# Graph attention on one core: q and k kept token by token, first loads amid the projections, keys loaded in eight parts

## The chip, the cores and the metric

The kernel runs on one core of a Trainium2 chip. The metric is the device time of one execution in microseconds (us), from the first to the last work of the core. A profiled execution gives the trace; its own time stands beside its span below, since all durations in the text come from it.

## The reference: what is computed

There are two layers on a graph of 2708 nodes with 128 features. Nearly all of the time goes into the first one, an attention whose 128 "batches" come from a plain reshape:

```python
q = (x @ Wq.T).reshape(d, n, h)        # d = 128, n = 2708, h = 8
k = (x @ Wk.T).reshape(d, n, h)
v = (x @ Wv.T).reshape(d, n, h)
a = jnp.einsum('dnh,dmh->dnm', q, k) * scale
a = a + spatial_encoding + edge_encoding   # both are adj
a = jax.nn.softmax(a, axis=2)
out = jnp.einsum('dnm,dmh->dnh', a, v).reshape(n, h * d)
x = _layernorm(x + out @ Wo.T)
```

Because of the reshape, batch d does not take one feature of every node. The projection's rows are laid end to end as 2708 x 128 rows of 8 numbers, and each batch takes 2708 consecutive ones, that is, rows of about 21 and a bit consecutive tokens. The second layer is a graph convolution, `adj @ (x @ W2) + b2` and once more with `W4`, with a residual and a layer norm.

## The kernel before

**Projections (L180 to L210).** The 2708 tokens go in 22 blocks of up to 128. For each block TensorE computes k, q and v (two matmuls of 512 columns each, L196). For k and q, ScalarE writes the value rounded to float32r (L205) and VectorE the rest, value minus rounded value (L206), so that both halves together keep the precision; the tile `pr` holds both. One DMA on SyncE's queue stores it (L208) into `ks` or `qs`. These DRAM tensors have 16 rows (8 numbers of the first half, 8 of the second) of 346624 = 2708 x 128 elements each, so that a token's data are 16 pieces of 128 elements, 512 bytes, far apart. v goes to `vs`, 4096 bytes in one piece per token (L201). For a later test of the range, VectorE takes the maximum and the minimum of each row (L210). The pool of `pr` has four buffers, so two blocks are under way.

**Attention (L213 to L443).** A group g is four of the 128 batches; there are 32 groups. In a group, the 2708 queries go in 6 blocks b of 452 (`QBS`), and for each block the 22 chunks of 128 keys are worked off in 9 steps (`plan`), for all four batches at once. A step has 2 to 4 pieces, each of two score tiles in the PSUM tile `s`, and three more score tiles in `p`. The engines share the work:

- TensorE makes the scores (L350, L347) and later multiplies the weights with the values and sums them up in `acc` (L371, L367).
- VectorE adds the adj column tile to `s` (L357), ScalarE takes the exponential of the sum (L443).
- For the tiles in `p`, ScalarE takes the exponential of the score alone (L440) and GpSimd multiplies with the exponential of adj (L441). That is computed once, in group 0 (L338), kept in DRAM (`near_exp`, stored at L339) and loaded afterwards (L328).
- At the end of a block VectorE copies `acc` to `o` (L377), and four DMAs store it (L379).

`interleave` lays out by hand which piece, sum or copy comes next, by times that it estimates; the order of instructions on each engine follows from it (`tc.manual_schedule()`). The projections lie outside of that and are ordered by the framework.

**Loads.** All DMAs are issued from SyncE's queue, in order; it stands still where one of them waits. At the start of each step, SyncE loads adj tiles until it is 8 tiles past what this step needs (L420). There are three kinds: `col` (one tile, 9 buffers), `two` (two tiles, two DMAs, 3 buffers) and `ecol` (7 buffers). Ahead of that, in the fourth step of a block (i == 3), come the 8 DMAs with the queries of the next block (`load_q`, L310; 16 rows each, so that both halves of k meet both halves of q). In step (b, i) = (1, 0) come the keys of the next group:

```python
def load_keys(g):
    t = raw.tile([P, N], F32R, tag="k_raw", name="k_raw")
    for j in range(GB):
        r0 = (GB * g + j) * N
        for i in range(4):
            nc.sync.dma_start(t[ds(32 * j + H * i, H), :].bitcast(F32), ks[ds(H * (i // 2), H), ds(r0, N)])
```

These are 16 DMAs of 8 rows. In step (2, 0) the values follow (`load_values`, 8 DMAs, L302 and L303). From block 2 on, GpSimd reorders them in pieces, one every other step: `order_keys` (L291, 8 pieces, and L295) and `spread_values` (L308). For group 0 all of this, with its memsets (L233 to L239), stands between the projections and the loop (L385 to L391).

**After the loop.** `layer0_out` divides, projects and normalises, and tests that all numbers lay in the range in which the exponentials need no maximum (L568, L569). If they did not, a branch at the end (L630) repeats the attention with maxima (`attention_with_maxima`); with these inputs it is not taken. `layer1` reads adj twice more.

Of the kernel before, what the change touches and what calls it, by code (L numbers as in the profile page):

```python
# [9 lines left out]
F32 = mybir.dt.float32  # L10
# [8 lines left out]
P = 128  # L19
# [110 lines left out]
def graph_attention_gcn(ctx: ExitStack, tc: tile.TileContext, x, xT, adj, adjT, adjP, adjS,  # L130
# [34 lines left out]

    qs = dram.tile([2 * H, R], F32, name="qs")
    ks = dram.tile([2 * H, R], F32, name="ks")
    vs = dram.tile([R, H], F32, name="vs")
# [3 lines left out]

    ends = const.tile([P, 2, 2, NM], F32, name="ends")
    nc.gpsimd.memset(ends, 0.0)

    with ExitStack() as s:
        wpool = s.enter_context(tc.tile_pool(name="wqkv", bufs=1))
        sb = s.enter_context(tc.tile_pool(name="proj", bufs=4))  # L180
        ps = s.enter_context(tc.tile_pool(name="ps_proj", bufs=4, space=PSUM))

        xT_sb = wpool.tile([P, N], F32, name="xT_sb")
        for i0, mi in ((0, P), (P, N - P)):
            nc.sync.dma_start(xT_sb[:, ds(i0, mi)], xT[:, ds(i0, mi)])
        w_sb = []
        for name, w in (("k", WkT), ("q", WqT), ("v", WvT)):
            t = wpool.tile([P, H * P], F32, name=f"w{name}_sb")
            nc.sync.dma_start(t, w)
            w_sb.append(t)  # L190
        v3 = vs.rearrange("(i g) e -> i (g e)", g=P)
        for c, (i0, mi) in enumerate(MC):
            for w, dst in zip(w_sb, (ks, qs, vs)):
                pp = ps.tile([P, 2, 512], F32, tag="pp", name="pp")
                for h in range(2):
                    nc.tensor.matmul(pp[:mi, h, :], xT_sb[:, ds(i0, mi)], w[:, ts(h, 512)], start=True, stop=True)  # L196
                flat = pp[:mi].rearrange("p a b -> p (a b)")
                if dst is vs:
                    o = sb.tile([P, H * P], F32, tag="po", name="po")
                    nc.scalar.copy(o[:mi], flat)  # L200
                    nc.sync.dma_start(v3[ds(i0, mi)], o[:mi])  # L201
                else:
                    f = half_scale if dst is qs else 1.0
                    o = sb.tile([P, 2, H * P], F32R, tag="pr", name="pr")
                    nc.scalar.mul(o[:mi, 0], flat, f)  # L205
                    nc.vector.scalar_tensor_tensor(o[:mi, 1], flat, f, o[:mi, 0].bitcast(F32), ALU.mult, ALU.subtract)  # L206
                    d3 = dst.rearrange("e (i g) -> i e g", g=P)
                    nc.sync.dma_start(d3[ds(i0, mi)], o[:mi].bitcast(F32).rearrange("p l (e g) -> p (l e) g", g=P))  # L208
                    for i, op in enumerate((ALU.max, ALU.min)):
                        nc.vector.tensor_reduce(ends[:mi, int(dst is qs), i, c : c + 1], o[:mi, 0].bitcast(F32), AX.X, op)  # L210


    with ExitStack() as s:  # L213
        kept = s.enter_context(tc.tile_pool(name="kept", bufs=1))
        raw = s.enter_context(tc.tile_pool(name="raw", bufs=1))
        kpool = s.enter_context(tc.tile_pool(name="kpool", bufs=2))
        qpool = s.enter_context(tc.tile_pool(name="qpool", bufs=3))
        cols = s.enter_context(tc.tile_pool(name="cols", bufs=9))
        twos = s.enter_context(tc.tile_pool(name="twos", bufs=3))
        ecols = s.enter_context(tc.tile_pool(name="ecols", bufs=7))  # L220
        epool = s.enter_context(tc.tile_pool(name="weights", bufs=4))
        ppool = s.enter_context(tc.tile_pool(name="products", bufs=4))
        opool = s.enter_context(tc.tile_pool(name="sums", bufs=2))
        ps = s.enter_context(tc.tile_pool(name="ps_s", bufs=2, space=PSUM))
        pq = s.enter_context(tc.tile_pool(name="ps_q", bufs=1, space=PSUM))
        pa = s.enter_context(tc.tile_pool(name="ps_a", bufs=1, space=PSUM))

# [47 lines left out]

        def load_keys(g):

            t = raw.tile([P, N], F32R, tag="k_raw", name="k_raw")
            for j in range(GB):
                r0 = (GB * g + j) * N  # L280
                for i in range(4):
                    nc.sync.dma_start(t[ds(32 * j + H * i, H), :].bitcast(F32), ks[ds(H * (i // 2), H), ds(r0, N)])
            groups[g] = kpool.tile([P, NU, P], F32R, tag="k", name="k"), k_short[g % 2], vals[g % 2], v_short[g % 2]
            raw_keys[g] = t

        def order_keys(g, i):

            t, (k, kz, _, _) = raw_keys[g], groups[g]
            if i < 8:
                n = P // 8  # L290
                nc.gpsimd.tensor_copy(k[:, :, ts(i, n)], t[:, ts(i, n * NU)].rearrange("p (q c) -> p c q", c=NU))  # L291
            else:
                for j in range(GB):
                    r = ds(32 * j, 32)
                    nc.gpsimd.tensor_copy(kz[r, ds(32 * j, SHORT)], t[r, ds(P * NU, SHORT)])  # L295

        def load_values(g):
            t = raw.tile([P, GB, NU * H], F32, tag="v_raw", name="v_raw")
            vz = v_short[g % 2]
            for j in range(GB):  # L300
                r0 = (GB * g + j) * N
                nc.sync.dma_start(t[:, j, :], vs[ds(r0, P * NU), :].rearrange("(p c) e -> p (c e)", c=NU))  # L302
                nc.sync.dma_start(vz[ds(32 * j, SHORT), ds(VW * j, H)], vs[ds(r0 + P * NU, SHORT), :])  # L303
            values[g] = t

        def spread_values(g, j):
            to = vals[g % 2].rearrange("p c (j e) -> p j c e", e=VW)
            nc.gpsimd.tensor_copy(to[:, j, :, :H], values[g][:, j, :].rearrange("p (c e) -> p c e", e=H))  # L308

        def load_q(g, b):  # L310
            n0, nw = QBS[b]
            q = qpool.tile([P, QB], F32R, tag="q", name="q")
            for j in range(GB):
                for i in range(2):
                    nc.sync.dma_start(q[ds(32 * j + 2 * H * i, 2 * H), :nw].bitcast(F32),  # L315
                                      qs[:, ds((GB * g + j) * N + n0, nw)])
            queries[g, b] = q

        def load_adj(n):
# [9 lines left out]
            else:  # L329
                t = adj_cols[g, b, m] = cols.tile([P, QB], F32, tag="col", name="col")  # L330
                m = -1 - m if m < 0 else m
                nc.sync.dma_start(t[:, :nw], adjP[ds(m * P, P), ds(n0, nw)])

        def first_exp(b, m):

            nw = QBS[b][1]
            t = ecols.tile([P, QB], F32, tag="ecol", name="ecol")
            nc.scalar.activation(t[:, :nw], adj_cols[0, b, -1 - m][:, :nw], AF.Exp, scale=2.0)  # L338
            nc.sync.dma_start(near_exp[b, m][:, :nw], t[:, :nw])  # L339
            exp_cols[0, b, m] = t  # L340

        def score(to, g, b, m, j):
            nw = QBS[b][1]
            k, kz, _, _ = groups[g]
            q = queries[g, b]
            if m == NU:
                nc.tensor.matmul(to[:, :nw], kz, q[:, :nw], start=True, stop=True)  # L347
            else:
                r = ds(32 * j, 32)
                nc.tensor.matmul(to[:, :nw], k[r, m, :], q[r, :nw], start=True, stop=True)  # L350

# [31 lines left out]
        s.enter_context(tc.manual_schedule())  # L383
        ahead, loaded = 8, 0
        load_keys(0)  # L385
        load_values(0)
        load_q(0, 0)
        for h in range(9):
            order_keys(0, h)
        for j in range(GB):  # L390
            spread_values(0, j)  # L391
        for what, n, c, beside in interleave(plan, len(steps) // len(plan), NU):
# [10 lines left out]
            if c == 0:  # L403
# [4 lines left out]
                if g + 1 < NG:  # L408
                    if (b, i) == (1, 0):
                        load_keys(g + 1)  # L410
                    elif (b, i) == (2, 0):
                        load_values(g + 1)
                    elif b > 1 and n % 2:
                        h = ((b - 2) * len(plan) + i) // 2
                        if h < 9:
                            order_keys(g + 1, h)
                        elif h < 9 + GB:
                            spread_values(g + 1, h - 9)
# [49 lines left out]
    nc.gpsimd.memset(reach, 1.0)  # L468
    fine = keep.tile([P, 7], F32, name="fine")

# [14 lines left out]
    def layer0_out(sb, ps, pa, judge):  # L485
# [72 lines left out]
        if judge:  # L558
# [4 lines left out]
            for i in range(2):  # L563
                limit = QK_LIMIT * (1.0, half_scale)[i]
                bounds += [(ends[:, i, 0, :], ALU.max, limit, ALU.is_le), (ends[:, i, 1, :], ALU.min, -limit, ALU.is_ge)]
            for i, (a, way, limit, op) in enumerate(bounds):
# [62 lines left out]
    rows_fine = nc.values_load(n_fine, min_val=0, max_val=P)  # L629
    with tc.If(rows_fine < P):  # L630
        with ExitStack() as t:
            attention_with_maxima(t, tc, qs, ks, vs, os_, adj, adjT, ident)
        rest(False)
# [127 lines left out]
```

## Time and profile before

| | us |
|---|---|
| median of 3 runs | 7105.78 |
| lowest and highest run | 7080.25, 7123.37 |
| the profiled execution's own time | 7111.18 |
| its span, first to last instruction | 7109.3 |
| first matmul starts | 8.79 |
| last store of the projections is issued, lands | 200.56, 205.10 |
| first add of the loop (VectorE, L357) starts | 232.62 |
| last copy `o` of the loop (L377) starts | 6771.7 |

The span thus has four stretches: the projections up to 205 us, 27.5 us up to the loop's first add, the loop up to about 6772 us, and some 337 us for the rest. The granted TensorE clock is 0.984 of full speed in the mean. DMA moves 1642.64 MB, 231 GB/s in the mean, in 1118588 packets.

The lines that follow in the prediction are read like this. In the page's first part, an engine has its busy time and share of the span. In its second part the span is cut into 40 slices, and each digit is the busy share in tenths. In the table by stretches, a row has the start and end, the length, the busy time of TensorE, its weight loads, VectorE, ScalarE and GpSimd (with the number of instructions), the granted clock, the mean share of the 16 DMA engines, and the rate. In the timeline a row has the start, the duration, the engine (SPq is SyncE's queue), the line of the kernel, the operation, and what is written from what.

### The profile page before, as it was taken

Reading aid. Unit: us, or ns where it says so; the run is one execution under the profiler, and the core shown is the slowest. Engines: PE = TensorE matmul, PEld = TensorE weight load, DVE = VectorE, ACT = ScalarE, POOL = GpSimd, SP = SyncE. Lnnn points to the kernel's source line nnn. Section 1 sums busy time; section 2 is a strip of 40 time slices with the busy share of each in tenths; the row PEclk is TensorE's granted clock in tenths of the full one; section 3 lists DMA queues with packets and bytes.
Section 4 is the critical chain, followed back from the end, with each engine's and each line's share of the span. In section 5 each row is a group of like instructions: output and inputs, shape, how many; then the busy total and the mean of one; then the engine's idle time right before and its main releaser. Section 6 shows DMA issues by size and latency. Waiting matters only on the chain.

```text
span 7109.3 us, 136670 instructions
## 1 busy us (share of the span) xinstructions
PE 6795.0 (96%) x50426; PEld 2165.0 (30%) x50426; DVE 6148.8 (86%) x6208; ACT 6549.0 (92%) x3659; POOL 5613.7 (79%) x2266
## 2 busy tenths in 40 slices
PE   6599999999999999999999999999999999999979
PEld 2122232323333233222322322223322222333354
DVE  7589999989999899888999988989988898999951
ACT  3699999999999999999999999999999999999920
POOL 0588888888888888888888888888888888888800
PEclk9799999999999999999999999999999999999999
DMA  9777767767766776777667776776667776677667
GB/s 287 224 246 234 233 223 237 245 221 231 236 225 230 236 242 223 227 235 228 222 229 236 242 221 221 232 228 227 229 226 232 230 237 221 226 237 232 227 189 233
DMA packets 1118588, 1642.64 MB, mean 231 GB/s; under 512 B 144373, under 2 KB 1083385, under 8 KB 1113685
## 3 DMA queue, kind: packets, MB, share of 16 engines
q1 hardware_dynamic: 1117908, 1633.81, 70.8%
q8 instruction: 399, 6.54, 0.4%
q14 instruction: 281, 2.29, 0.1%
HBM read 1551.44 MB, written 81.80 MB: 230 GB/s over the span
## 4 chain that ended last, share of the span: by engine, by line
PE 45%; DMA 16%; ACT 11%; DVE 8%; POOL 8%; issue 8%; SPq 3%; DVEq 0%; ACTq 0%; POOLq 0%
PE acc L371 22%; PE s L350 15%; POOL w L441 8%; DVE e L357 7%; ACT e L443 6%; DMA col<-in_adjP 6%; ACT w L440 4%; DMA ecol<-ne 4%; PE acc L588 3%; DMA k_raw<-ks 2%; DMA two<-in_adjP 2%; PE p L350 2%; PE acc L367 2%; SPq L315 1%; DMA ks<-pr 1%
## 5 line engine op out<-in xcount | busy, mean ns | idle before, releaser
L441 POOL TENSOR_TENSOR w<-w,ecol 128x1356 f32<-128x1356 f32 (+1 forms) x1728 | 5351.1, 3103 | 934.4 <-ACT w L440 845.0
L357 DVE TENSOR_TENSOR e<-s,col 128x904 f32<-128x904 f32 (+1 forms) x4608 | 4829.6, 1091 | 499.1 <-PE s L350 182.8
L443 ACT ACTIVATE e<-e 128x2712 f32<-128x2712 f32 (+5 forms) x1728 | 4709.0, 2725 | 2.6 <-DVE e L357 2.5
L371 PE MATMUL acc<-e,vals 128*32 128x452 f32 x21888 | 3844.9, 558 | 11.5 <-ACT e L443 0.6
L350 PE MATMUL s<-q,k 32*128 32x452 f32 x10944 | 2468.4, 468 | 188.8 <-DVE e L357 79.6
L440 ACT ACTIVATE w<-p 128x1356 f32<-128x1356 f32 (+1 forms) x1728 | 2395.4, 1386 | 78.4 <-PE p L350 72.9
L350 PEld LDWEIGHTS s<-q,k 32*128 32x128 f32 x10944 | 1027.4, 183 | 3360.5 <-DVE e L357 2846.9
L371 PE MATMUL acc<-w,vals 128*32 128x452 f32 x10368 | 1671.9, 559 | 0.0
L350 PE MATMUL p<-q,k 32*128 32x452 f32 (+1 forms) x5184 | 1273.4, 439 | 13.3 <-ACT w L440 13.1
L357 DVE TENSOR_TENSOR e<-s,two 128x904 f32<-128x904 f32 (+1 forms) x960 | 1047.6, 1091 | 182.8 <-ACT w L440 80.6
L371 PEld LDWEIGHTS acc<-e,vals 128*32 128x32 f32 x21888 | 621.6, 108 | 857.5 <-issue 789.7
L350 PEld LDWEIGHTS p<-q,k 32*128 32x128 f32 x5184 | 521.4, 183 | 31.9 <-ACT w L440 31.0
L371 PEld LDWEIGHTS acc<-w,vals 128*32 128x32 f32 x10368 | 280.3, 108 | 205.1 <-issue 178.1
L291 POOL CAST k<-k_raw 128x336 fp32r<-128x336 f32 x256 | 225.7, 883 | 13.2 <-DMA v_raw<-vs 13.2
L367 PE MATMUL acc<-e,v_short 128*128 128x452 f32 (+1 forms) x384 | 196.7, 594 | 0.0
L233 POOL MEMSET k_short<- 128x128 f32 x2 | 0.3, 204 | 203.9 <-DMA vs<-po 203.9
L205 ACT ACTIVATE pr<-pp 128x1024 fp32r<-128x1024 f32 (+1 forms) x44 | 45.0, 1023 | 116.0 <-DMA ks<-pr 55.5
L377 DVE COPY o<-acc 128x452 f32<-128x452 f32 x192 | 118.5, 617 | 6.2 <-PE acc L371 6.2
L588 PE MATMUL acc<-col,xw 128*128 128x512 f32 (+2 forms) x264 | 105.6, 549 | 0.0
L588 PE MATMUL acc<-col,hw 128*128 128x512 f32 (+2 forms) x264 | 104.1, 545 | 0.0
L210 DVE TENSOR_REDUCE ends<-pr 128x1 f32<-128x1024 f32 (+1 forms) x88 | 102.7, 1207 | 0.0
L480 ACT ACTIVATE sd<-mv,eps 128x1 f32<-128x1 f32 (+1 forms) x22 | 5.9, 291 | 104.7 <-DVE mv L474 104.7
(77 smaller groups left out, 980.4 us busy)
## 6 DMA issues: line engine op xcount, KB each, us to landing
col<-in_adjP SPq DMA_DIRECT2D x1965, 226.0 KB
two<-in_adjP SPq DMA_DIRECT2D x1440, 226.0 KB
ecol<-ne SPq DMA_DIRECT2D x1395, 226.0 KB
col<-in_adjP SPq DMA_DIRECT2D x393, 224.0 KB
two<-in_adjP SPq DMA_DIRECT2D x288, 224.0 KB
ecol<-ne SPq DMA_DIRECT2D x279, 224.0 KB
col<-in_adjT SPq DMA_DIRECT2D x210, 256.0 KB
k_raw<-ks SPq DMA_DIRECT2D x512, 84.6 KB
```

The costliest lines, as they stand in the source:

```text
L210: nc.vector.tensor_reduce(ends[:mi, int(dst is qs), i, c : c + 1], o[:mi, 0].bitcast(F32), AX.X, op)
L291: nc.gpsimd.tensor_copy(k[:, :, ts(i, n)], t[:, ts(i, n * NU)].rearrange("p (q c) -> p c q", c=NU))
L315: nc.sync.dma_start(q[ds(32 * j + 2 * H * i, 2 * H), :nw].bitcast(F32), qs[:, ds((GB * g + j) * N + n0, nw)])
L350: nc.tensor.matmul(to[:, :nw], k[r, m, :], q[r, :nw], start=True, stop=True)
L357: nc.vector.tensor_add(e[:, ds(at, 2), :nw], st[:, :, :nw], a)
L367: nc.tensor.matmul(a[:, :nw], vz, e[:, t, :nw], start=False, stop=False)
L371: nc.tensor.matmul(a[ds(32 * j, VW), :nw], v[:, m, ds(VW * j, VW)], e[:, t, :nw], start=(m == first_chunk), stop=(m == last_chunk))
L377: nc.vector.tensor_copy(o[:, :nw], acc.pop((g, b))[:, :nw])
L440: nc.scalar.activation(w[:, :, :nw], sp[:, :, :nw], AF.Exp, scale=2.0)
L441: nc.gpsimd.tensor_mul(w[:, :, :nw], w[:, :, :nw], exp_cols[g, b, two][:, :nw].unsqueeze(1).to_broadcast([P, 3, nw]))
L443: nc.scalar.activation(e[:, :at, :nw], e[:, :at, :nw], AF.Exp, scale=2.0)
L588: nc.tensor.matmul(acc[:, :nw], src[:mw, m, :], t[:mw, :nw], start=(m == 0), stop=(last is None and m == NM - 1))
```

## The change

In words:

- `qs` and `ks` become `[N, 16, 128]`: each token's 16 pieces lie together, 8192 bytes. The projection stores a token in one piece.
- The loads of k and q read whole tokens, from the one that holds the first wanted row to the one that holds the last (`whole_tokens`). They read 16 or 8 pieces of 512 bytes per token and put the tokens side by side, shifted so that the wanted part begins at element 128 of the tile. The tiles grow: `k_raw` from 2708 to 24 x 128 elements per partition, `q` from 452 to 768. `qpool` goes from three buffers to two.
- Group 0's keys (8 parts, blocks 2 to 9), its first queries and its values (blocks 10 to 13), and its first eight adj tiles (blocks 14 to 17) are loaded inside the projections' loop; GpSimd's reordering for group 0 follows there too, and the memsets come ahead of the projections. The loop begins with `loaded = ahead`, 8. The pools `weights`, `products`, `sums` and the PSUM pools open after the projections' pools have closed.
- In later groups the keys come in eight parts of two DMAs, in steps 0 to 7 of block 1; the values in four parts, in steps 0, 2, 4 and 6 of block 2.
- For the range test, one reduction of absolute values takes the place of maximum and minimum, and two bounds the place of four.
- The first 128 columns of xT and the weights are loaded ahead of the rest of xT.
- The branch that is not taken first copies `qs` and `ks` into the old layout.

```diff
-    qs = dram.tile([2 * H, R], F32, name="qs")
-    ks = dram.tile([2 * H, R], F32, name="ks")
+    qs = dram.tile([N, 2 * H, P], F32, name="qs")
+    ks = dram.tile([N, 2 * H, P], F32, name="ks")
...
-        qpool = s.enter_context(tc.tile_pool(name="qpool", bufs=3))
+        qpool = s.enter_context(tc.tile_pool(name="qpool", bufs=2))
...
+        def whole_tokens(r0, n):
+            return ds(r0 // P, (r0 % P + n - 1) // P + 1), r0 % P
+
+        def load_keys(g, h):
+            if h == 0:
+                groups[g] = kpool.tile([P, NU, P], F32R, tag="k", name="k"), k_short[g % 2], vals[g % 2], v_short[g % 2]
+                raw_keys[g] = raw.tile([P, NM + 2, P], F32R, tag="k_raw", name="k_raw")
+            tokens, off = whole_tokens((GB * g + h // 2) * N, N)
+            flat = raw_keys[g].rearrange("p t g -> p (t g)")
+            n = tokens.size
+            for i in (2 * h, 2 * h + 1):
+                to = flat[ds(H * i, H), ds(P - off, n * P)].bitcast(F32)
+                nc.sync.dma_start(to.rearrange("p (t g) -> p t g", g=P),
+                                  ks[tokens, ds(H * (h % 2), H), :].rearrange("t e g -> e t g"))
...
+        def load_q(g, b, js=range(GB)):
...
+            for j in js:
+                tokens, off = whole_tokens((GB * g + j) * N + n0, nw)
+                n = tokens.size
                 for i in range(2):
-                    nc.sync.dma_start(q[ds(32 * j + 2 * H * i, 2 * H), :nw].bitcast(F32),
-                                      qs[:, ds((GB * g + j) * N + n0, nw)])
+                    to = queries[g, b][ds(32 * j + 2 * H * i, 2 * H), ds(P - off, n * P)].bitcast(F32)
+                    nc.sync.dma_start(to.rearrange("p (t g) -> p t g", g=P), qs[tokens].rearrange("t r g -> r t g"))
...
+            nc.sync.dma_start(xT_sb[:, :P], xT[:, :P])
...
+            nc.sync.dma_start(xT_sb[:, P:], xT[:, P:])
...
-                    d3 = dst.rearrange("e (i g) -> i e g", g=P)
-                    nc.sync.dma_start(d3[ds(i0, mi)], o[:mi].bitcast(F32).rearrange("p l (e g) -> p (l e) g", g=P))
-                    for i, op in enumerate((ALU.max, ALU.min)):
-                        nc.vector.tensor_reduce(ends[:mi, int(dst is qs), i, c : c + 1], o[:mi, 0].bitcast(F32), AX.X, op)
+                        nc.sync.dma_start(dst.rearrange("i r g -> i (r g)")[ds(i0, mi)],
+                                          o[:mi].bitcast(F32).rearrange("p l f -> p (l f)"))
+                        nc.vector.tensor_reduce(ends[:mi, int(dst is qs), c : c + 1], o[:mi, 0].bitcast(F32), AX.X,
+                                                ALU.max, apply_absolute_value=True)
+
+                if 2 <= c < 10:
+                    load_keys(0, c - 2)
+                elif 10 <= c < 10 + GB:
+                    load_q(0, 0, [c - 10])
+                    load_values(0, c - 10)
+                elif 10 + GB <= c < 10 + GB + ahead // 2:
+                    load_adj(2 * (c - 10 - GB))
+                    load_adj(2 * (c - 10 - GB) + 1)
+            for h in range(9):
+                order_keys(0, h)
+            for j in range(GB):
+                spread_values(0, j)
...
-                    if (b, i) == (1, 0):
-                        load_keys(g + 1)
-                    elif (b, i) == (2, 0):
-                        load_values(g + 1)
-                    elif b > 1 and n % 2:
+                    if b == 1 and i < 2 * GB:
+                        load_keys(g + 1, i)
+                    elif b == 2 and i % 2 == 0 and i < 2 * GB:
+                        load_values(g + 1, i // 2)
+                    if b > 1 and n % 2:
...
-                bounds += [(ends[:, i, 0, :], ALU.max, limit, ALU.is_le), (ends[:, i, 1, :], ALU.min, -limit, ALU.is_ge)]
+                bounds.append((ends[:, i, :], ALU.max, limit, ALU.is_le))
```

## The prediction

> **What bounds the kernel now.** I read the page's totals and slices first, then busy time by stretches, then the order of VectorE's copies L377 (one per group and query block, so a clock of the loop), then SyncE's queue.
>
> ```profile
> PE 6795.0 (96%) x50426; PEld 2165.0 (30%) x50426; DVE 6148.8 (86%) x6208; ACT 6549.0 (92%) x3659; POOL 5613.7 (79%) x2266
> ...
> ACT  3699999999999999999999999999999999999920
> ```
>
> TensorE and ScalarE are full nearly everywhere; the holes are at the start and the end. The stretches (PE, PEld, DVE, ACT, POOL busy, granted clock, DMA share, GB/s):
>
> ```profile
> 20.00:190.00 170.00, 116.71 (x244) 43.66 (x242) 139.19 (x122) 60.60 (x61) 0.00 (x0) 0.96 0.96 296
> 205.20:217.00 11.80, 0.00 (x0) 0.00 (x0) 0.00 (x0) 0.00 (x0) 6.14 (x14) 0.50 0.48 80
> 217.00:226.00 9.00, 0.00 (x0) 0.00 (x0) 0.00 (x0) 0.00 (x0) 0.90 (x2) 0.50 0.52 88
> 516.40:555.50 39.10, 35.63 (x260) 10.17 (x255) 30.87 (x32) 34.35 (x19) 28.91 (x11) 0.91 0.79 254
> 555.50:588.70 33.20, 32.73 (x260) 9.91 (x255) 30.58 (x31) 33.20 (x19) 30.83 (x14) 1.00 0.67 226
> ```
>
> The projections are bound by DMA (0.96). From 205 to 226 no compute engine but GpSimd works: the first loads stand bare. An ordinary block is bound by compute (PE 32.73 and ACT 33.20 of 33.20). The block in which the next group's keys are loaded (516 to 555) is 6 us longer, with both engines idle for part of it. The copies say how often that happens:
>
> ```profile
> 482.93 0.61 DVE L377 COPY o<-acc 128x448 f32<-128x448 f32 x1
> 516.39 0.62 DVE L377 COPY o<-acc 128x452 f32<-128x452 f32 x1
> 555.46 0.62 DVE L377 COPY o<-acc 128x452 f32<-128x452 f32 x1
> 588.71 0.62 DVE L377 COPY o<-acc 128x452 f32<-128x452 f32 x1
> 621.79 0.62 DVE L377 COPY o<-acc 128x452 f32<-128x452 f32 x1
> ```
>
> Over all 192 copies, the second block of groups 1 to 30 lasts 36.44 us in the mean (33.23 to 41.21), the other blocks 33.1 to 33.4; in group 31, which loads no keys, it lasts 33.40. So the excess goes with the key loads: 30 x (36.44 - 33.34) = **93 us**. In group 0 that block lasts 53.45 against 37.54 for the next: 16 us more; ScalarE's timeline there has one hole of 11.55 us that ends with an adj column's landing. SyncE shows why:
>
> ```profile
> 501.12 10.86 SPq L282 DMA_DIRECT2D k_raw<-ks  x16
> 512.47 0.35 SPq L332 DMA_DIRECT2D col<-in_adjP  x1
> ...
> 520.52 2.28 SPq L379 DMA_DIRECT2D os<-o  x4
> 523.16 4.48 SPq L315 DMA_DIRECT2D q<-qs  x8
> ```
>
> For 10.9 us no adj column is issued. In the chain of waits eight key issues follow each other by 0.34 us and the ninth waits for a landing: eight transfers are in flight at a time.
>
> [...] Eight rows use eight engines; the trace agrees (share 0.48 while key loads run alone). The new key loads still have eight rows. [...] The trace agrees in direction: its packet records have the 512-byte writes of ks and qs at 27 ns (18.9 bytes per ns), the 4096-byte writes of vs at 191 ns mean, 171 median (21.5 to 24). [...] the trace agrees for SyncE's queue too (L379 waits 1215.5 us in all for the copy o). [...]
>
> **The change, part by part**, against the profiled execution: span 7109.3, its own time 7111.18, so 2 us lie around the span; the median of the runs is 7105.78, 5 us lower.
>
> 1. *Projection writes.* A 128-token block lasts 8.72 us now (ks issues at 65.54 and 74.22, 82.89, 91.62). Per DMA engine it is 256 packets of 512 bytes at 27 ns = 6.91 and 8 of 4096 bytes at 191 = 1.53: 8.44. After, q and k are 16 packets of 8192 bytes; none of that kind is in the trace as a write, so it is bounded: 27 ns per 512 bytes as now (no gain) up to 24 bytes per ns, 5.5 us (gain 1.4 per block). I take the mean rate of the 4096-byte writes, 21.5: 6.1 us, block 7.6 + 3% = 7.8 us, gain 0.9 x 21.2 = **-19**. ScalarE (3.05) and VectorE (2 x (1.22 + 2.33) = 7.1, after the change 2 x (1.22 + 1.17) = 4.8) stay below that, so the 44 reductions saved are worth nothing here. If the writes took under 4.8 us, VectorE would be the bound.
> 2. *Weights before most of xT.* The first weights land at 8.66 us behind 1354 KB of xT. The 1290 KB now come last; at 290 GB/s that is 4.5 us less ahead of the first matmul, but the DMA has to move all of it before the writes run freely: I take **-2.5** (0 to -4).
> 3. *First loads amid the projections.* From the last write's landing (205.1) to VectorE's first add (232.62) lie 27.5 us. They go; their DMA work moves into the writes' stretch. Keys: 16 transfers x 22.1 packets per engine on eight engines. 512-byte reads are priced by the loads ot<-os: 27 ns median, 29.4 mean (27464 packets). 354 x 29.4 = 10.4 us. q: 8 x 4.5 x 29.4 ns = 1.1; v: 4 x 8 x 38 ns (672-byte reads) = 1.2; eight adj tiles, ten or so transfers x 8 x 80 ns = 6.4. Together **+19** on the busiest engines, beside nothing, since DMA is the bound there. GpSimd's casts and memsets (6.6 + 0.9 + 1.1 and 6.5 us) lie on an idle engine; if that cover failed they would cost 8.6. SyncE stands in front of the next writes whenever one of these loads waits for a write to land; blocks 2 to 9 need only the first block's tokens, long landed. If the wait is for the newest write instead, 2 to 4 us a block over up to 12 blocks: 0 to +40, I take **+1**. Sum of the start: -19 - 2.5 - 27.5 + 19 + 1 = **-29** (0 to -47). The loop's first block starts with eight tiles loaded where ScalarE now idles about 4 us between 233.8 and 248: **-2** (0 to -4).
> 4. *Keys in eight parts.* 2 transfers in each of eight steps of 3.7 us, in place of 16 at once. SyncE: about 3.4 adj transfers x 0.47 + 2 x 0.5 = 2.6 us a step, it fits. Queued behind them are the step's adj columns, and VectorE's adds and GpSimd's products wait for those. Engines 0 to 7 in that block: 260 adj packets x 75 to 84 ns = 19.5 to 21.8, keys 354 x 27 to 29.4 = 9.6 to 10.4, q 1.0: 30 to 33 us of 33.3. Full, but the loop loads eight tiles ahead (2.7 steps, 10 us, less about 4 for a landing = 6 us of slack). The tightest place is the fourth step: os (2.3), q (4.5), two key parts (1.2) = 8.0 us without an adj column, where other blocks have 6.8 and lose nothing. I leave 0.5 us a group (0 to 1.5): -93 + 15 = **-78** (-47 to -93), and for group 0, where near_exp is written too, -12 of the 16 (-6 to -16).
> 5. *q as whole tokens.* 4.5 packets of 512 bytes per row for one of 1808: 8 x (4.5 x 29.4 - 84) ns = 0.4 us more DMA per block, where the share is 0.67: hidden; if it were not, 77 us over 192 blocks. Two buffers for three: SyncE reaches a q load just after the wait for the previous block's copy o (520.52, then 523.16), when the older block's scores are done: nothing. Values in four parts in place of one: today's block with v loads is not longer (33.30), nothing.
> 6. *Range test.* Two fewer pairs of 0.17 + 0.15 us: **-0.6**. The branch's new copies are not executed.
>
> Sum: -29 - 2 - 78 - 12 - 0.6 = -121.6; 7111.2 - 121.6 = 6989.6. I say **6990**, 1.7% below.
>
> **Rivals.** *Engines 0 to 7 stay short* (chance 0.14): the parts spread the shortage instead of ending it, 1.5 us a group remain, 6 in group 0: -29 - 2 - 47 - 10 = -88, 7023. For it: the 33 of 33.3 above. Against: 5 of 30 groups take the burst itself with no loss.
> *The start gives nothing* (0.12): 8192-byte packets run no faster, or loads hold SyncE in front of writes: start 0, loop as forecast: -92, 7019. For it: no such write is in the trace.
> *Strided 512-byte reads are dear* (0.05), the slower side: reads at a pitch of 8 KiB take 65 ns. Keys 354 x 65 = 23.0, q 2.3, adj 21.8: 47.1 us on engines 0 to 7, 13.8 too much, less 6 of slack = 7.8 a group against 3.1 today: +141; group 0 +5; start -29 + 13 - 2 = -18: 7239. It decides from about 55 ns, where the loss eats the start's gain. Against it: 29.4 ns in ot<-os, 512-byte rows too, though at another pitch.
> The forecast's own case has 0.69.
>
> **How the numbers follow.** The forecast's own ends are -161 (7111 - 47 - 4 - 93 - 16 - 1 = 6950) and, with both first rivals at once, 7111 - 47 - 6 = 7058. Runs differ by 20 us either way. I give 6940 to 7050; above it lie the dear reads and part of the rivals together. 0.5% (36 us) is about what a measurement of this kernel can tell from no change. Faster by more than that: 0.69 + 0.12 + 0.08 = 0.89; within: 0.06; slower: 0.05.
>
> **What would show it.** Right: packets of 8192 bytes below 400 ns and a block period near 7.8 us; VectorE's first add near 203; the second block's mean at 33.8 or less in groups 1 to 30; 512-byte reads below 32 ns. Wrong: a second block still above 35 us; SyncE standing between writes in the projections; read packets above 55 ns; or a hole after the fourth step's q loads.

## The result and the profile after

The change makes the kernel slower. The median is 7284.68 us (7280.82 to 7296.58, 4 runs) against 7098.18 before (7080.25 to 7123.37, 4 runs), a ratio of 1.0263 with a 95% interval of 1.0227 to 1.0299. The profiled execution took 7296.58 us with a span of 7294.7, 185.4 longer than before's span.

The lines that answer to those of before are these. First the page's totals and ScalarE's slices (PE is TensorE, PEld its weight loads, DVE VectorE, ACT ScalarE, POOL GpSimd):

```profile
PE 6909.4 (95%) x50426; PEld 2174.4 (30%) x50426; DVE 6099.8 (84%) x6160; ACT 6565.2 (90%) x3659; POOL 5614.6 (77%) x2266
...
ACT  4999999999999999999999999999999999999930
```

The totals move little (TensorE's by 114 us, of which more below), and in slices of 182 us nothing is seen but a shorter start. The busy time by stretches tells more: a part of the projections, then the second block of group 1, then the block after it.

```profile
20.00:150.00 130.00, 109.44 (x234) 41.39 (x232) 86.00 (x75) 56.59 (x56) 8.70 (x16) 0.99 0.98 385
450.00:494.20 44.20, 36.50 (x260) 10.39 (x255) 30.94 (x32) 34.86 (x19) 29.73 (x11) 0.88 0.87 175
494.20:527.70 33.50, 32.83 (x260) 9.90 (x255) 30.55 (x31) 32.79 (x19) 30.02 (x14) 1.00 0.78 267
```

The projections store at 385 GB/s in place of 296. But the second block now lasts 44.20 us, with ScalarE and VectorE about as busy as in the next one, so that ScalarE is idle for 9.3 us of it; the DMA engines are busy for 0.87 of it and move only 175 GB/s. Busy engines that move little are the sign to look for. The waits of that block (who waited for whom: us in total, times, longest) name what is late:

```profile
PEld s L374 <- DVE e L381: 24.2, 21, 4.1
ACT w L457 <- PE p L374: 9.2, 2, 5.0
DVE e L381 <- DMA col<-in_adjP: 6.4, 2, 3.6
```

ScalarE waits for scores, TensorE's scores wait for VectorE's adds, and the adds wait for adj columns. TensorE also loses in a second way: its 260 matmuls take 36.50 us in this block and 32.83 in the next, at a granted clock of 0.88 in place of 1.00. Five microseconds of the block show it:

```profile
485.00:490.00 5.00, 5.00 (x30) 0.94 (x22) 2.68 (x3) 2.82 (x2) 1.72 (x2) 0.61 1.00 229
```

TensorE is busy for all of this stretch, at a clock of 0.61, while ScalarE works for 2.82 us of it. In the clock records of groups 1 to 30, TensorE stands at half speed for 13.9 us per second block in the mean (3.8 before), and in no other block. How much of the longer block is the lower clock and how much the wait for adj was not separated.

VectorE's copies of `acc`, in the timeline, show that it is this block and no other:

```profile
416.50 0.61 DVE L401 COPY o<-acc 128x448 f32<-128x448 f32 x1
449.97 0.62 DVE L401 COPY o<-acc 128x452 f32<-128x452 f32 x1
494.16 0.62 DVE L401 COPY o<-acc 128x452 f32<-128x452 f32 x1
527.70 0.62 DVE L401 COPY o<-acc 128x452 f32<-128x452 f32 x1
```

Over the run, the second block of groups 1 to 30 lasts 44.92 us in the mean (41.05 to 47.32; before 36.44), their other blocks 33.31 (before 33.32), and group 31's second block, without key loads, 33.42. The account of the 185 us: the first copy comes at 212.9 in place of 279.3, **-66**; 30 second blocks x (44.92 - 36.44) = **+254**; the other blocks and the end come to about -3 (from the last copy to the end of the span it is 337.6 us before and 337.7 after).

SyncE's queue in such a block:

```profile
646.01 0.88 SPq L249 DMA_DIRECT2D k_raw<-ks  x2
647.25 0.36 SPq L300 DMA_DIRECT2D col<-in_adjP  x1
647.86 0.89 SPq L293 DMA_DIRECT2D two<-in_adjP  x2
649.08 0.33 SPq L296 DMA_DIRECT2D ecol<-ne  x1
649.71 1.88 SPq L249 DMA_DIRECT2D k_raw<-ks  x2
```

The parts lie between the adj columns as planned, and no part holds the queue for long. What is slow is the transfer behind the issue: the packet records have the queries' 512-byte packets at 27 ns, as priced, but the keys' at about 67 in the mean, and the 1808-byte packets of adj in that block at 132 (90 before). With adj at 75 ns, the median of its packets over the loop, the eight engines that carry keys (an estimate: the share was 0.48 while key loads ran alone before; the records do not number the engines) have 354 x 67 ns = 23.7, q 1.0, adj 278 x 75 = 20.9, together 45.6 us, close to the block's 44.9. This sum is no proof: with the 132 ns that the adj packets took it would be 61 us, and packets overlap in the records (in the bare loads below, the share of 16 engines is up to 1.19).

### The profile page after: what moved, and what is told of

It is laid out like the page before. It is cut to its first block, busy times and chain, and to the rows that moved or that the text cites. A ratio compares the mean times of both kernels' runs of the same rounds, so it can differ in the third digit from the quotient of the medians.

```text
span 7294.7 us, 136614 instructions
## 1 busy us (share of the span) xinstructions
PE 6909.4 (95%) x50426; PEld 2174.4 (30%) x50426; DVE 6099.8 (84%) x6160; ACT 6565.2 (90%) x3659; POOL 5614.6 (77%) x2266
## 4 chain that ended last, share of the span: by engine, by line
PE 45%; DMA 23%; ACT 8%; DVE 8%; POOL 7%; issue 7%; SPq 4%; DVEq 0%; POOLq 0%; ACTq 0%
PE acc L395 22%; PE s L374 15%; DMA col<-in_adjP 7%; POOL w L458 7%; DVE e L381 7%; DMA k_raw<-ks 6%; ACT e L460 5%; DMA two<-in_adjP 3%; DMA ecol<-ne 3%; PE acc L605 3%; ACT w L457 3%; SPq L285 2%; PE p L374 2%; PE acc L391 1%; DMA qs<-pr 1%
## 5 line engine op out<-in xcount | busy, mean ns | idle before, releaser
L395 PE MATMUL acc<-e,vals 128*32 128x452 f32 x21888 | 3931.4, 572 | 12.1 <-ACT e L460 0.5
L457 ACT ACTIVATE w<-p 128x1356 f32<-128x1356 f32 (+1 forms) x1728 | 2363.5, 1368 | 313.8 <-PE p L374 284.6
L374 PE MATMUL p<-q,k 32*128 32x452 f32 (+1 forms) x5184 | 1304.3, 447 | 11.0 <-ACT w L457 10.8
L332 DVE SCALAR_TENSOR_TENSOR pr<-pp,pr 128x1024 fp32r<-128x1024 f32 (+1 forms) x44 | 53.8, 1222 | 57.5 <-ACT pr L331 56.1
```

The lines of the kernel that those rows point to most:

```text
L374: nc.tensor.matmul(to[:, :nw], k[r, m, :], q[r], start=True, stop=True)
L395: nc.tensor.matmul(a[ds(32 * j, VW), :nw], v[:, m, ds(VW * j, VW)], e[:, t, :nw], start=(m == first_chunk), stop=(m == last_chunk))
L457: nc.scalar.activation(w[:, :, :nw], sp[:, :, :nw], AF.Exp, scale=2.0)
```

## The experiments

In the following, "second block" is the mean over groups 1 to 30, and packet times are means of the trace's packet records around that block; the queries' packets, about 27 ns, are taken out. A time without a number of runs is that of a single execution; single executions of the kernel before lay between 7076 and 7128 us. Theory A: the memory's pitch. B, later P: the place of the rows in SBUF. C: cutting the burst into parts as such. D: the number of engines. Eight engines for a DMA of 8 rows and 16 for one of 16 are estimated from the share of the DMA engines in the bare loads below: 0.55 to 0.61 with 8 rows, 1.12 to 1.19 with 16.

**The source: pitch.** Only the distance of tokens in `ks` changes.

```diff
-    ks = dram.tile([N, 2 * H, P], F32, name="ks")
+    ks_wide = dram.tile([N, (2 * H + 1) * P], F32, name="ks")
+    ks = ks_wide[:, : 2 * H * P].rearrange("n (r g) -> n r g", g=P)
```

> The changed kernel with the tokens of ks 8704 bytes apart instead of 8192; all packets keep their sizes. In the changed kernel the second block of groups 1 to 30 lasts 44.9 us and the packets of the keys take about 67 ns. Theory A (eight engines that read at a pitch of 8 KiB hit the same part of the memory): packets of the keys near 30 ns, second block 33.5 to 35.5, time 6980 to 7010. Theory B (the SBUF side: eight engines write small packets into eight neighbouring partitions): no change, 44 to 46, 7285. Theory C (the eight parts as such take SyncE's lead): no change, 7285.

Measured: 7290.69 us, second block 44.64, key packets 67 ns. In the timeline of VectorE, group 1's second block lies between the second and the third copy:

```profile
448.97 0.62 DVE L402 COPY o<-acc 128x452 f32<-128x452 f32 x1
496.16 0.62 DVE L402 COPY o<-acc 128x452 f32<-128x452 f32 x1
```

With 8704 bytes from token to token it is as with 8192. The pitch is not the cause; theory A falls.

**The parts and the layout, each alone.** In the first kernel `ks` goes back to 16 long rows, and the eight parts stay:

```diff
-                nc.sync.dma_start(to.rearrange("p (t g) -> p t g", g=P),
-                                  ks[tokens, ds(H * (h % 2), H), :].rearrange("t e g -> e t g"))
+                nc.sync.dma_start(to, ks[ds(H * (h % 2), H), ds(r0, N)])
```

> The changed kernel with ks alone put back into 16 long rows, so that each key row is one packet of 10832 bytes; still in eight parts, q stays token by token. Theory A: second block 33.5 to 36, time 6990 to 7060 (the 512-byte writes of ks cost the start about 20 us). Theory B: much the same, since the packets are large: 34 to 37. Theory C: the block stays at 43 to 46, about 7300.

Measured: 7176.07 us, second block 40.30, key packets (10832 bytes) 885 ns against 699 before, adj packets 122 ns. In the second kernel the layout stays, and the burst comes back:

```diff
-                    if b == 1 and i < 2 * GB:
-                        load_keys(g + 1, i)
+                    if (b, i) == (1, 0):
+                        for part in range(2 * GB):
+                            load_keys(g + 1, part)
```

> The changed kernel with all 16 key DMAs in step (1, 0), as before; layout as changed. Theories A and B: the packets stay dear, second block 44 to 48 us, time 7270 to 7380. Theory C: second block back at 36.4, time about 7030.

Measured: 7160.16 us, second block 40.19, key packets 50 ns, adj packets 90 ns. No theory had expected this: with the kernels before and after, the four make a square in which both steps cost (the kernel before differs in its queries, values and stores too). The parts add 3.9 us with long rows (36.44 to 40.30) and 4.7 with tokens (40.19 to 44.92); the layout adds 3.8 in a burst and 4.6 in parts.

**The destination.** The source, the sizes and the number of packets stay; only the partitions change.

```diff
-                to = flat[ds(H * i, H), ds(P - off, n * P)].bitcast(F32)
+                to = flat[i :: 2 * H, ds(P - off, n * P)].bitcast(F32)
```

> The changed kernel with each key DMA's eight rows written to partitions 16 apart (i, i+16, ... i+112) instead of eight neighbours; source, sizes and number of packets are unchanged. Keys' rows then stand on other partitions, so the scores are sums over other pairs of rows. Theory A: no change, second block 44 to 46, 7285. Theory B: packets near 30 ns, second block 33.5 to 35.5, time about 6990. Theory C: no change.

Measured: 7096.01 us, second block 38.32, key packets 48 ns. This is the largest step so far, 6.6 us a block, from nothing but the place where the rows land. It comes although each issue now holds SyncE for longer. One issue's shortest, median and longest time in ns, in the changed kernel and here:

```profile
L249 SPq DMA_DIRECT2D k_raw<-ks x512: 271/293/1235, 26.9 to 6610.0; - x171
L249 SPq DMA_DIRECT2D k_raw<-ks x512: 567/602/1387, 25.6 to 6405.4; - x171
```

Theory B holds in kind; the 33.5 to 35.5 that it expected was missed.

**Bare loads.** What key loads cost by themselves, in the changed kernel with extra loads ahead of the loop (one of the four sets, each issued twice):

```diff
+            for i in range(16):
+                nc.sync.dma_start(wide[ds(H * i, H)], ks[tokens, :H, :].rearrange("t e g -> e t g"))
```

> The changed kernel with four sets of extra key loads, issued twice between the projections and the loop, of no use to the result: 16 DMAs of 8 rows to neighbouring partitions; 16 of 8 rows to partitions 16 apart; 8 of 16 rows to neighbours; 8 of 16 rows to partitions 8 apart. All are bare, 22 or 23 packets of 512 bytes per row. Theory D: 8 rows cost the same near or far, 27 to 32 ns a packet, 10 to 12 us a set; 16 rows half of that. Theory B: neighbours 55 to 70 ns, 20 to 25 us a set; apart 27 to 32 ns, 10 to 12 us; 16 neighbours 10 to 13 us; 16 apart 5 to 7 us. The sets together lengthen the run by 60 to 110 us.

Measured: 7401.89 us. The second round of the sets in the busy time by stretches (the last two columns are the share of 16 DMA engines and GB/s): 8 rows to neighbours, 8 rows 16 apart, 16 rows to neighbours, 16 rows 8 apart.

```profile
218.30:242.10 23.80, 0.00 (x0) 0.00 (x0) 0.00 (x0) 0.00 (x0) 0.00 (x0) 0.50 0.61 60
243.60:258.80 15.20, 0.00 (x0) 0.00 (x0) 0.00 (x0) 0.00 (x0) 0.00 (x0) 0.50 0.58 95
260.50:273.40 12.90, 0.00 (x0) 0.00 (x0) 0.00 (x0) 0.00 (x0) 0.00 (x0) 0.50 1.19 112
276.20:284.10 7.90, 0.00 (x0) 0.00 (x0) 0.00 (x0) 0.00 (x0) 0.00 (x0) 0.50 1.12 195
```

(The last rate is 185 without the first adj column, whose load begins there.) The packets take 82, 49, 86 and 46 ns. All sets move the same 1.44 MB with no compute beside them, and their rates differ by a factor of three: rows that stand apart in place of neighbours take it from 60 to 95 GB/s with 8 rows and from 112 to 185 with 16. One number does not fit a rate that the place alone sets: the first round of 8 rows to neighbours ran at 111 GB/s, in 13 us. In that set DMAs that follow each other go to different partitions, so engines that are out of step could write to more of them at once; this explanation was not tested.

**Sixteen rows on sixteen engines.** The parts of `ks` are stored so that a DMA can take all 16 rows of a token, and q's rows take every second partition, so that every product of halves is still formed.

```diff
-            for i in (2 * h, 2 * h + 1):
-                to = flat[ds(H * i, H), ds(P - off, n * P)].bitcast(F32)
...
+            to = flat[ds(2 * H * h, 2 * H), ds(P - off, n * P)].bitcast(F32)
+            nc.sync.dma_start(to.rearrange("p (t g) -> p t g", g=P), ks[tokens].rearrange("t r g -> r t g"))
```

> The changed kernel with keys loaded in 16-row DMAs: a token's rows of ks are stored first half and rest in turn, a DMA takes all 16 to 16 neighbouring partitions, one DMA in each of the eight steps; q's rows go to every second partition so that all four products of halves are kept. Twice the engines, half the DMAs, same bytes in SBUF. Theory D (the sum of the packets on the eight engines that carry the keys is the limit: 278 adj packets x 75 ns + 354 key packets x 67 ns = 44.6 us): per engine 177 key packets, 20.9 + 5 to 12 = 26 to 33 us, so the second block falls to 33.3 to 34.5 and the time to 6930 to 6970. Theory B (narrow destination on the SBUF side): packets stay at 60 ns or more in neighbours, block 34 to 37, time 6960 to 7050. Theory C (the parts as such cost 4 us): block 37 to 38, time about 7060.

Measured: 7126.86 us (15 runs), ratio to before 1.0033 (1.0023 to 1.0043), second block 38.29. This is above the ranges of theories D and B and just above that of C. The block is 6.6 us shorter, as much as with the better destination on eight engines (38.32); in the bare sets, too, 16 rows to neighbours (112 GB/s) and 8 rows 16 apart (95) lie close. How much is the engines' and how much that of the 16 partitions in place of 8 is not told apart here. And something is lost elsewhere, as in all three runs here that step q's rows: the eight issues of a block's queries take 5.4 us in place of 4.0, and the blocks without key loads last 33.70 in place of 33.31, some 58 us over the run. The same kernel with all eight DMAs at once:

> The kernel with 16-row key loads, but all eight DMAs in step (1, 0). Theory D: 8 DMAs in 4 to 6 us are inside SyncE's lead, block 33.3 to 34.5, no difference from the eight parts. Theory C: the burst is better than the parts by some 4 us a block. If the lead of eight tiles is what a burst eats: 35 to 36.

Measured: 7159.24 us, second block 39.16, key packets 72 ns (47 in parts), adj packets 87. Theory D had expected 33.3 to 34.5 for both, and theory C a burst that gains 4 us; here it gains nothing.

**Steps within 32 partitions, with eight engines and with 16.** That they would help more than rows 16 apart was the author's estimate. In the next kernel, 8-row DMAs on eight engines go to every fourth partition of their 32:

```diff
-                to = flat[ds(H * i, H), ds(P - off, n * P)].bitcast(F32)
+                to = flat[first + i : first + 32 : 4, ds(P - off, n * P)].bitcast(F32)
```

> Key loads with eight rows on eight engines as in the changed kernel, same number and sizes of packets, but the rows go to every fourth partition of their 32[...]; q's rows go to every second partition and its halves are stored in turn so that all products are kept. Theory P: packets 27 to 35 ns, 20.9 + 354 x 31 ns = 32 us, second block 33.5 to 36, time 6940 to 7020. Theory D: the engines are the limit, 38 to 45 us, 7090 to 7285.

Measured: 7090.89 us (12 runs), ratio 0.9988 (0.9974 to 1.0001), second block 36.70, key packets 33 ns. From 44.92 to 36.70 with the same eight engines: the block lies between the ranges of theories P and D, the time at the edge of D's. That the whole does no better than the kernel before has to do with the other blocks: q's rows are stepped here too, the blocks without key loads last 33.66, and 150 x 0.35 = 53 us are lost there. What is left in the second block can be the eight engines (354 x 33 ns + 20.9 + 1.0 = 33.7 us of work, by the rough sum above, in a block that should take 33.3) or SyncE: in group 1 it issues `os`, q and keys for 9.0 us without an adj column, against 7.0 in the next kernel. This run does not tell them apart. In the last step, q's rows go back to neighbours, and the keys' 16 rows go to every second partition:

```diff
+            first = 32 * (h // 2)
+            to = flat[first + h % 2 : first + 32 : 2, ds(P - off, n * P)].bitcast(F32)
+            nc.sync.dma_start(to.rearrange("p (t g) -> p t g", g=P), ks[tokens].rearrange("t r g -> r t g"))
```

> 16-row key loads in eight parts as in the run with 16 rows, but the keys' rows go to every second partition of their 32 and q's rows to neighbours (the order of halves in DRAM is exchanged between q and k)[...]. Theory P ([...] the bare sets gave 61, 95, 112 and 185 GB/s[...]): packets near 46 ns at worst, 20.9 + 8 = 29 us of 33.3, second block 33.3 to 35, time 6930 to 6990. Theory D (only the number of engines counts): as with 16 neighbours, 38 us, 7125.

Measured: **6949.42 us** (6939.59 to 6950.94, 5 runs), ratio to before **0.9791** (0.9773 to 0.9810), second block 33.64, key packets 39 ns. This version beats both kernels. Its second block of group 1 and the block after it, by stretches:

```profile
424.90:458.30 33.40, 32.94 (x260) 10.11 (x255) 30.68 (x31) 33.40 (x19) 28.75 (x11) 1.00 0.83 232
458.30:492.00 33.70, 33.05 (x260) 10.05 (x255) 30.69 (x32) 33.64 (x19) 31.11 (x14) 1.00 0.78 258
```

ScalarE is busy for all 33.40 us of the block with the key loads, at a clock of 1.00; nothing of the stall is left. Theory P had expected this. The bare sets to every second and every fourth partition were run too:

> The changed kernel with six bare sets of loads of no use, issued twice between projections and loop: 16 DMAs of 8 rows with 512-byte packets to neighbours, to every second and to every fourth partition; 8 DMAs of 16 rows to every second; 16 DMAs of 8 rows of 10832 bytes (from vs) to neighbours and to every fourth partition. Theory P: 80, 48 and 27 to 35 ns a packet; 16 rows 46 ns; the long rows 1000 ns to neighbours, 450 to 600 to every fourth. Theory D: 8 rows cost the same in all three, about 80 ns.

Measured: 7423.58 us. Second round, 8 rows to neighbours, to every second, to every fourth, 16 rows to every second; each stretch lies within the set's own transfers:

```profile
232.00:248.00 16.00, 0.00 (x0) 0.00 (x0) 0.00 (x0) 0.00 (x0) 0.00 (x0) 0.50 0.61 82
250.00:261.00 11.00, 0.00 (x0) 0.00 (x0) 0.00 (x0) 0.00 (x0) 0.00 (x0) 0.50 0.60 116
262.00:271.00 9.00, 0.00 (x0) 0.00 (x0) 0.00 (x0) 0.00 (x0) 0.00 (x0) 0.50 0.55 144
272.50:279.50 7.00, 0.00 (x0) 0.00 (x0) 0.00 (x0) 0.00 (x0) 0.00 (x0) 0.50 1.16 189
```

In the first round they ran at 111, 141, 131 and 188 GB/s. The packets of the second round took 59, 43, 31 and 48 ns in the mean, in the order that theory P gave. 8 rows to every fourth partition give 131 and 144 GB/s, at 31 ns a packet, close to the 27 of the queries, so there the engines may be the limit; 16 rows to every second give 188 and 189, at an engine share of 1.16 in place of 0.55. Plain distance is not the reason: 16 rows 8 apart and 16 rows 2 apart run at 185 and 189, and 8 rows 4 apart run faster (131 and 144) than 8 rows 16 apart (95). What it is in the rows' place that counts is not shown. Not all sets are steady, either: 8 rows to neighbours gave 60 to 111 GB/s over four rounds, to every second partition 116 and 141. The long rows to every fourth partition took about 540 ns in both rounds, those to neighbours about 1150 in the first and 520 in the second. So the place of one DMA's rows does not fix the rate of several in flight.

**What the parts are worth once the loads are wide.** The fast version with its eight key DMAs at once:

> The kernel with 16-row key loads to every second partition, but all eight DMAs in step (1, 0). Bare, such a set takes 5.5 us. Theory E (a burst starves the loop only where it outlasts SyncE's lead): 5.5 us is inside the lead of some 8, so the second block stays at 33.4 to 34.5 and the time at 6940 to 6970; the parts as such are then worth nothing. Theory F (a burst always costs, the parts are what ends the stall): block 35.5 to 38, time 7010 to 7080.

Measured: 6941.74 us (4 runs), ratio 0.9790 (0.9769 to 0.9811), second block 33.46. Theory E holds: with and without parts there is no clear difference (7.7 us between the medians, and the runs overlap). This burst, whose eight issues for group 1's keys take 5.43 us, does no harm.

**The start.** The fast version with group 0's loads after the projections:

> The kernel with 16-row key loads to every second partition in eight parts, but with group 0's keys, values, queries and adj tiles loaded after the projections, as before. Tells apart what the moved loads and what the long packets of the stores gave to the start, which came out 66 us shorter in all. If the move gave the 25 us that the bare loads took: first add 18 to 25 us later than with the loads amid (157), so 175 to 182, time 6970 to 6975. If the long packets gave nearly all: first add by 165, time 6955.

Measured: 6953.12 us (4 runs), ratio 0.9803 (0.9783 to 0.9824); VectorE's first add is at 167.07 in place of 156.97. So the move gives 10 us there, since the wide key loads (5.35 us for their issue, where before's took 11.27) leave little to hide. This is near the second expectation: most of the gain of the start came from the stores and the shorter loads, not from the move. The medians of the whole differ by 3.7 us. Without loads amid them, the stores of `ks` of one block and the next are 6.5 us apart, where it was 8.7 before.

## Why the prediction was wrong

The sign is wrong. The step that failed is part 4, in its term for engines 0 to 7, "keys 354 x 27 to 29.4 = 9.6 to 10.4". It measured 354 x 67 ns = 23.7 us. The price came from the loads `ot<-os`, which also are 512-byte reads, but into 128 partitions; the key loads put eight rows on eight neighbouring partitions. With the same packets on eight engines, the rows' place alone moved the packets from 67 to 48 ns and the block from 44.92 to 38.32. The prediction has no term for the destination, though the bare key loads before, at 80 GB/s with an engine share of 0.48, pointed to one. Nor has it one for the granted clock, which was 0.88 in group 1's second block and 1.00 in the next. The fast version shows that the room that part 4 counted on is there: with 16 rows to every second partition, the excess of the second block is 0.3 us, where 0.5 was allowed.

- *The rival of dear reads* had 65 ns a packet and 7239 us, and was given 0.05. That its price was right is luck, since its mechanism was wrong: the pitch changes nothing (67 ns a packet at 8704 bytes as at 8192). It also left out that adj packets are slowed (90 to 132 ns in the changed kernel); it expected 41.1 us for the block, and it was 44.9.
- *The two likelier rivals.* "Engines 0 to 7 stay short" named the right block, but left 1.5 us a group, and it was 11.6. "The start gives nothing" did not happen: the start gave 66 us.
- *Eight parts.* Forecast as the cure (-78). With 8 rows to neighbours they make it worse by 4 to 5 us a block, with 16 rows to neighbours they do not (38.29 in parts, 39.16 in a burst), with wide loads they change nothing. Why they harm is not shown. The author's estimate: in a burst eight key DMAs are in flight and go to several sets of partitions, in parts only two, and adj packets for those same partitions are held up. For it speak the key packets (50 ns in the burst, 67 in parts) and the adj packets (90 and 132); against it, that with 16 rows to neighbours the key packets are slower in the burst (72 ns, 47 in parts). It was not tried by itself and stays open.
- *Stores of the projections.* The direction was right, the size too small: 8192-byte packets took 317 ns, not 381, and the 4096-byte ones 172, not 191. Per block 16 x 0.317 + 8 x 0.172 = 6.4 us against 8.44, so -43 rather than -19; the 6.5 us between stores without loads amid them agree. The long rows of `ks` alone (first add at 186.15 against 166.26 with tokens) were worth 20 us, which fits half of it.
- *The start as a whole* was forecast at -31 with the first block and came at -66. The first store comes 3.0 us earlier (14.89 to 11.86), where 2.5 was said. SyncE stood for some 15 us in all before a load of keys or queries until a store had landed (9.4 us of it for `qs`), where +1 was taken; how much of this delayed a store is open. How the remaining 20 us split between hidden loads and their DMA work was not measured in the changed kernel itself.
- *Group 0's second block*: forecast -12, measured 53.60 against 53.45, for the same reason as above; 37.69 in the fast version. (The block after it lasts 37.64 us before; the 37.54 of the prediction is the one after that.)
- *q as whole tokens, two buffers, values in parts, range test*: nothing, as forecast. The queries' packets take 27 ns, and blocks without key loads last 33.31 us against 33.32.

## What to carry to other kernels

The size of its packets did not price a DMA into few neighbouring partitions: 512-byte packets took 27 ns for the queries' 16 rows and 67 for the keys' 8, and 48 for 8 rows 16 apart. Take a packet's duration only from a DMA to the same set of partitions. Where a load must go to a few rows, step them over the partitions and give it 16 rows; here that was worth 335 us against the same change without it. Stepping lengthened the issue (the median from 0.29 to 0.60 us for 8 rows of keys, from 0.42 to 0.59 for q's 16), so step the rows that need it and no others: in the runs with q's rows stepped, the blocks without key loads lost 40 to 58 us in all. Where a transfer stalls a loop, make it short first: here, with 8 rows to neighbours, the block was longer in parts than in a burst (44.92 us against 40.19), and so were the adj packets beside them (132 ns against 90).

## What was not expected of the hardware

- The same 1.44 MB in 512-byte packets went into SBUF at 60 to 189 GB/s, by the place of the rows and their number in a DMA, 8 or 16; and 8 rows to neighbours alone at 60 to 111, from round to round.
- Packets of one transfer are longer beside others: the adj packets took 132 ns in the mean beside narrow key loads in parts, 104 beside wide ones, 82 in a block without keys.
- From 20 to 150 us, the projections with their stores in 8192-byte packets ran at 403 GB/s in the run without loads amid them (385 in the changed kernel and 411 in the fast version, with loads), against 297 before, with most packets of 512 bytes.
- In groups 1 to 30, TensorE's granted clock fell only in the blocks that load keys: 13.9 us at half speed per block in the changed kernel, 3.8 before, none in the fast version.
- The issue of a DMA took twice as long when its 8 rows went to partitions 16 apart (0.60 us, against 0.29 to neighbours).
